# One maximum instruction for the last two score banks, the first keys' bias in the held copy, and the time step's maximum on ScalarE, in a perceiver layer on one core

## Chip, cores and metric

The kernel runs on one core of a Trainium2 chip. The metric is the device time of one execution in microseconds. Profiles are of one execution each. PE is TensorE (PEld its weight loads), DVE is VectorE, ACT is ScalarE, POOL is GpSimd, and SP issues the DMAs.

## The reference, cut to what matters

One perceiver layer in fp32: 16 sequences of 128 queries, width 512, each with a context of 2048 rows. It has three parts, each with a residual sum.

```
# 1. cross attention: 16 heads of 32
q = layernorm(x) @ wq.T + bq;  k = ctx @ wk.T + bk;  v = ctx @ wv.T + bv
attn = softmax(q k^T / sqrt(32));  x = x + (attn @ v) @ wo.T + bo
# 2. a Mamba block (width 1024, 16 states, 128 time steps) and a GELU MLP
dt = softplus(dt_low @ dt_proj_w.T + dt_proj_b)
h  = exp(dt * A) * h + dt * B * xa      # scan over time
# 3. a small mixture of experts
```

What the change touches: the softmax's maxima over the scores, the bias bk of the keys, and softplus, which the kernel computes as max(t, 0) + log(1 + exp(-|t|)) with t = the projection plus its bias.

## The kernel before

**Steps.** The attention runs in 256 steps u (loop at L1329). A step takes one block of 512 context rows of one sequence and one group of four heads: `split(u)` gives the sequence u // 16, the block u // 4 % 4 and the head group u % 4. Its scores are four matmuls (`scores`, L302), one head each, into four PSUM banks of 128x512, `banks[0..3]` (L129). The other four PSUM banks are `avp` (attention sums), `hst` (scan), `pa` and `pc` (products for keys and values).

**Softmax.** `maxima` (L312) reduces each bank on DVE (L315) into one column of its own tile `nm`, and `exps` (L319) follows on ACT with one exponential a bank (L325), which takes the negated maximum as its bias and also sums the row. The maxima are local to a block and are joined at a sequence's end (`joined`, L460). The probabilities of banks 0 and 1 are transposed on PE into the same two banks (`turn`, L353, matmuls at L357) and copied out by ACT (L359); those of banks 2 and 3 are transposed on DVE in blocks (`blocks`, L337) and put in order by DMA through DRAM (L341, L347). The next step's `weighted` (L385) multiplies them with the values.

**Keys and values** of the next block are made in the same steps from seven quarter products (`product`, L244) in place of eight. In step u with u % 4 equal to 1 or 2 it is keys, else values, each in two phases. `x_products` fills `pa` and `pc`. `hold` (L285) copies `pa` to SBUF on ACT; `x_sums` adds `pc` to the held copy on DVE (L264 for keys, with the bias bk, one instruction for each of the two head groups r; L274 for values). Then `y_products` (one product in phase 0, two in phase 1) adds to `pa` and `pc`, and `y_sums` holds or sums again; the fourth quarter is a sum on ACT (L262, bias and copy).

**The scan** of a group of two sequences runs beside later sequences' attention, from step 54 on. `dt_first` (L662) makes the time step of a block of 128 channels in every fourth step, u % 4 = 3, behind the products: a matmul (L665), Abs and Exp on ACT (L669, L670), the maximum on DVE (L672), a sum on POOL. `decays` (L719) are exponentials on ACT into `hst`, half of them before the maxima and half after the held copy; `scan` (L734, L735) runs on DVE and POOL.

**Order.** Each engine's order is the order of the calls in the loop; nothing rearranges it. Waits are put in by tile: a write to a tile waits for the last reads of it, whichever part these read. In a step the order is: half of the decays; scores; `weighted` of the step before; maxima; `x_products`; exps; POOL's work; first scan; hold; second half of the decays; blocks; `x_sums`; `turn` for banks 0 and 1; second scan (before the late work in even steps, after it in odd ones); late work; `y_products` and `y_sums`; work put behind.

**Late work** (L1421 to L1443) is a list of functions that need a PSUM bank for a while, such as `scaled` (L499: spreads the softmax's sums over the partitions by transposes at L502, then a product on DVE at L507 or L509; two in the step with u % 16 = 3 and two with u % 16 = 4), `x_part` and `z_part` (L581, L602: the Mamba input projection, matmuls at L577, one of each in eight steps of 32), `x_proj` (L631), `projected` (L762), `turned` (L429, transposes at L432) and `queries`. They get bank 2 first, then bank 3, then bank 0. A single late item in steps with u % 16 = 3 or 10 is put ahead of `turn` (L1430), into bank 2.

From step 256 on no attention is left: the last scans go on beside the MLP and the experts of the sequences already done, then these alone.

Of the kernel before, what the change touches and what calls it, by code (L numbers as in the profile page):

```python
# [19 lines left out]
SB = S // 512  # L20
# [12 lines left out]
NP = 4 - ND  # L33
# [3 lines left out]
def perceiver_layer(ctx: ExitStack, tc: tile.TileContext, a: dict, out: bass.AP):  # L37
    nc = tc.nc
# [74 lines left out]
    with ExitStack() as es:  # L113
        acon = es.enter_context(tc.tile_pool(name="acon", bufs=1))
        keep = es.enter_context(tc.tile_pool(name="keep", bufs=2))
        ssm = es.enter_context(tc.tile_pool(name="ssm", bufs=2))
        psum = es.enter_context(tc.tile_pool(name="psum", bufs=1, space=PSUM))
        att = es.enter_context(ExitStack())
        pool = att.enter_context(tc.tile_pool(name="att", bufs=2))
# [6 lines left out]

        banks = [psum.tile([P, 512], FP, tag=f"s{j}", name=f"bank{j}") for j in range(4)]  # L129
        avp = psum.tile([P, 4, P], FP, tag="av", name="avp")  # L130
        hst = psum.tile([P, NH // 2, GT], FP, tag="h0", name="hst")
        pa = psum.tile([P, 2, 256], FP, tag="pa", name="pa")
        pc = psum.tile([P, 2, 256], FP, tag="pc", name="pc")

        bq = acon_in("bq", [P, KC])
        bk = acon_in("bk", [P, KC])
# [116 lines left out]
        def k_sum(g, o, c, pc, x):  # L253
            for r in range(2):
                hg = 2 * o + r
                if (g, hg) not in kts:
                    kts[g, hg] = pool.tile(
                        [P, 512], FP, tag=f"kt{hg}", name=f"kt{g}_{hg}", bufs=1 + (hg == 3)
                    )
                t = kts[g, hg][:, c * 256 : (c + 1) * 256]  # L260
                if pc is None:
# [17 lines left out]
            for i, ps in (((1, pa), (2, pc)), ((7, pa), (5, pc)))[ph]:  # L279
                product(of, g, i, ps)  # L280

        def hold(key, g, pa, tag):
            n = ND if tag == "tr" else 1
            t = pool.tile([P, 2 * n, 256], FP, tag=tag, name=f"{tag}{key}{g}", bufs=1)[:, 0:2, :]
            nc.scalar.copy(t, pa)  # L285
            held[key] = t

        def x_sums(of, g, ph, pa, pc):
# [5 lines left out]

        def y_sums(of, g, ph, pa, pc, tag="u2"):
            if ph == 0:
                hold(of + "u2", g, pa, tag)
            else:
                sums[of](g, 0, 1, pc, held[of + "u2"])
                sums[of](g, 1, 0, None, pa)  # L300

        def scores(u):  # L302

            b, sb, hg = split(u)
            for j in range(4):
# [4 lines left out]
            del kts[u // 4, hg]  # L310

        def maxima(u):  # L312
            b, sb, hg = split(u)
            for j in range(4):
                nc.vector.tensor_reduce(  # L315
                    stats[b][0][j][:, sb, hg : hg + 1], banks[j], AX.X, ALU.max, negate=True
                )

        def exps(u):  # L319
            b, sb, hg = split(u)  # L320
            nm, sm = stats[b]
            pr = pool.tile([P, 4, 512], FP, tag="pr", name=f"pr{u}", bufs=1)
            for j in range(4):
                h = hg * 4 + j
                nc.scalar.activation(  # L325
                    pr[:, j, :],
                    banks[j],
                    AF.Exp,
                    bias=nm[j][:, sb, hg : hg + 1],
                    accum_out=sm[:, sb, h : h + 1],  # L330
                )
            prs[u] = pr
# [81 lines left out]
        def normal(b):  # L414

            x = xts[b]
            root_third(rstd[:, b : b + 1], *xts.pop((b, "r")))
            xn = keep.tile([P, D], FP, tag="aT", name="xn", bufs=1)
            nc.vector.tensor_scalar(
                xn, x, mv[:, b, 0:1], rstd[:, b : b + 1], ALU.subtract, ALU.mult  # L420
            )
            if b:
                nc.gpsimd.tensor_tensor(x, x, bo, ALU.add)
            xts[b, "n"] = xn
            nm = [keep.tile([P, SB, 4], FP, tag=f"nm{j}", name=f"nm{b}_{j}") for j in range(4)]
            sm = keep.tile([P, SB, H], FP, tag="sm", name=f"sm{b}")
            stats[b] = nm, sm

# [31 lines left out]
        def joined(b):  # L460

            parts, sm = stats[b]
            nm = keep.tile([P, SB, H], FP, tag="nm", name=f"nm{b}")
            for j in range(4):
                nc.vector.tensor_copy(
                    nm.rearrange("p s (k j) -> p s k j", j=4)[:, :, :, j], parts[j]
                )
            stats[b] = nm, sm

        def joined_first(b):  # L470
# [191 lines left out]
        def dt_first(g, ec, ps):  # L662

            ps = ps[:, 0:GT]
            nc.tensor.matmul(ps, dtw, xd, start=True, stop=True)  # L665


            e = ssm.tile([P, GT], FP, tag="e", name="e", bufs=1)
            nc.scalar.activation(e, ps, AF.Abs, bias=dtb[:, ec : ec + 1])  # L669
            nc.scalar.activation(e, e, AF.Exp, scale=-1.0)  # L670
            dt = ssm.tile([P, GT], FP, tag="dt", name="dt")
            nc.vector.tensor_scalar(dt, ps, dtb[:, ec : ec + 1], 0.0, ALU.add, ALU.max)  # L672
            u = ssm.tile([P, GT], FP, tag="u", name="u", bufs=1)
            nc.gpsimd.tensor_scalar(u, e, 1.0, 1.0, ALU.mult, ALU.add)
            dts[g, ec] = dt, e, u
# [124 lines left out]
        def flat(ps):  # L800
            return ps.rearrange("p k q -> p (k q)")
# [6 lines left out]
        def give_back(*ps):  # L808
            free_banks.extend(ps)
# [466 lines left out]

        def first_sums(of, ph):
            sa, sc = dict((w[0], w[1:3]) for w in ways)[of]
            hold(of, 0, sa, "u1")
            x_sums(of, 0, ph, sa, sc)  # L1280

        load_factors("k", 1, ("a11",))
# [46 lines left out]
        for u in range(last):  # L1329
# [47 lines left out]
            if u == NU:  # L1377
                weighted(NU, range(NP, 4))
                weighted_last(u - 1)
                att.close()  # L1380
                give_back(*banks, flat(avp))
                open_ffn()
            if u == NU + 8:
# [22 lines left out]
            if live and u % 4 == 2:  # L1406
                values_kept(u // 4)
            if makes:
                hold(of, made, pa, "u1")
            if scans:  # L1410
                decays(g, r, 1)
            if live:
# [6 lines left out]


            after_turns = late.get(u, ())  # L1421
            free = banks[NP:]
            places = [(free + banks)[i] for i in range(len(after_turns))]
            if live and len(after_turns) > len(free):
                if u % 4 == 0:
                    places = [flat(avp), *places[:-1]]
                elif u % 2 and makes and u not in behind:
                    places[-1] = flat(pc)
# [110 lines left out]
```

## Time and profile before

| | us |
|---|---|
| median of 3 runs | 3578.6 (3576.97 to 3579.74) |
| the profiled execution | 3579.3 |
| its span, first to last instruction | 3577.5 |
| PE busy | 3518.9 |
| DVE busy | 2672.0 |
| POOL busy | 2462.7 |
| ACT busy | 2285.5 |
| 1024 maxima of a bank (L315), mean of one | 0.678 |
| 1024 exponentials of a bank (L325), mean of one | 0.684 |
| held copies (L285), 128x512, mean of one | 0.58 to 0.60 |
| sums of keys (L264), 128x256, mean of one | 0.46 to 0.48 |
| sums of values (L274), 128x512, mean of one | 0.66 to 0.69 |
| the time step's maximum (L672), 128x256, mean of one | 0.476 |

The granted TensorE clock is 0.995 of full speed. The steps 0 to 255 begin at 43.1 us and the last begins at 2888.1 us.

How to read it: a line of the timeline gives the start in us from the span's start, the duration, the engine, the source line, the operation, the tiles (out<-in), the shapes and, with x, how many follow each other; in brackets stands how long the engine sat idle before and what released it. Matmuls are pipelined and their ends are modelled, so the row of a matmul reaches into the next one. A line of the table of windows gives a stretch, its length, and the busy time and instructions of PE, PEld, DVE, ACT and POOL, then the granted clock, the DMA share and the DMA rate.

### The profile page before, as it was taken

The numbers are of one execution on the slowest core, as the hardware profiler recorded it, in microseconds if no ns is written. First come the engines' busy times: TensorE is split into PE (matmuls) and PEld (weight loads), VectorE is DVE, ScalarE is ACT, GpSimd is POOL, SyncE is SP. The second block draws the span as 40 slices with busy tenths as digits, with TensorE's granted clock in tenths as the row PEclk, the third lists the DMA queues.
The fourth block names the chain that finished last, engine by engine and source line by source line (L and its number), as shares of the span: only waits on it lengthen the run. The fifth ranks groups of instructions, "written<-read, shape, count | busy, mean of one in ns | idle before, by whom it ended". The sixth has DMA issues, their size and how long they took to land.

```text
span 3577.5 us, 68547 instructions
## 1 busy us (share of the span) xinstructions
PE 3518.9 (98%) x24072; PEld 2638.5 (74%) x24072; DVE 2672.0 (75%) x4390; ACT 2285.5 (64%) x5672; POOL 2462.7 (69%) x2353
## 2 busy tenths in 40 slices
PE   8999999999999999999999999999999989999999
PEld 6777787778777877787778777877777756656655
DVE  4555556897889788978797879887988767668743
ACT  3555556777677766777677767776777665545422
POOL 2111214896889788978797779777987778789920
PEclk9999999999999999999999999999999999999999
DMA  4444445787788778787788778778777887676742
GB/s 146 159 148 154 159 152 193 250 265 220 254 251 268 233 253 256 252 243 247 250 257 247 231 257 265 240 224 271 254 245 224 266 300 254 219 273 245 260 173 77
DMA packets 527541, 816.79 MB, mean 228 GB/s; under 512 B 44848, under 2 KB 378960, under 8 KB 526944
## 3 DMA queue, kind: packets, MB, share of 16 engines
q1 hardware_dynamic: 526752, 811.79, 70.4%
q8 instruction: 192, 3.15, 0.3%
q14 instruction: 149, 1.22, 0.1%
q0 software_dynamic: 448, 0.63, 0.1%
HBM read 661.51 MB, written 150.73 MB: 227 GB/s over the span
## 4 chain that ended last, share of the span: by engine, by line
PE 86%; DVE 4%; POOL 4%; DMA 3%; ACT 3%; issue 1%; SPq 0%; DVEq 0%; POOLq 0%
PE pa L244 24%; PE pc L244 17%; PE bank L307 7%; PE avp L385 7%; PE bank L577 6%; PE bank L357 6%; PE bank L986 3%; PE bank L762 3%; PE bank L955 2%; PE bank L1087 2%; PE bank L515 2%; ACT pr L325 1%; POOL w L698 1%; DMA bc<-bcd 1%; PE bank L442 1%
## 5 line engine op out<-in xcount | busy, mean ns | idle before, releaser
L325 ACT ACTIVATE pr<-bank,nm 128x512 f32<-128x512 f32 x1024 | 688.5, 684 | 199.3 <-DVE nm L315 197.3
L315 DVE TENSOR_REDUCE nm<-bank 128x1 f32<-128x512 f32 x1024 | 633.8, 678 | 60.0 <-PE bank L307 59.6
L698 POOL TENSOR_TENSOR w<-dx,bc 128x512 f32<-128x512 f32 x512 | 648.1, 1287 | 30.7 <-DMA bc<-bcd 22.6
L749 POOL TENSOR_TENSOR ysum<-ysum,w 128x512 f32<-128x512 f32 x384 | 500.4, 1303 | 229.4 <-DVE hst L712 205.9
L719 ACT ACTIVATE hst<-dt,alog 128x254 f32<-128x254 f32 x918 | 442.4, 482 | 71.5 <-DVE hst L712 39.1
L337 DVE STREAM_TRANSPOSE tr<-pr 128x1024 f32<-128x1024 f32 x256 | 318.8, 1245 | 119.9 <-ACT pr L325 110.3
L735 POOL TENSOR_TENSOR w<-w,bc 128x512 f32<-128x512 f32 x256 | 329.1, 1286 | 76.6 <-DVE w L734 74.0
L385 PEld LDWEIGHTS avp<-pT,v 128*32 128x32 f32 x4096 | 204.4, 110 | 198.3 <-issue 194.2
L734 DVE TENSOR_TENSOR_SCAN w<-hst,w 128x512 f32<-128x512 f32 x256 | 309.5, 1209 | 40.0 <-ACT hst L719 33.2
L236 POOL TENSOR_TENSOR t<-c,c 128x512 f32<-128x512 f32 x128 | 164.3, 1283 | 232.3 <-PE pc L244 135.6
L359 ACT COPY pT<-bank 128x512 f32<-128x512 f32 x512 | 271.7, 581 | 48.9 <-PE bank L357 48.8
L307 PE MATMUL bank<-kt,qT 32*128 32x512 f32 x2048 | 301.3, 641 | 1.6 <-ACT pT L359 1.6
L385 PE MATMUL avp<-pT,v 128*32 128x128 f32 x4096 | 276.4, 277 | 1.5 <-ACT pT L359 1.4
L357 PE MATMUL bank<-ident,pr 128*128 128x128 f32 x2048 | 266.2, 273 | 0.8 <-ACT pr L325 0.7
L357 PEld LDWEIGHTS bank<-ident,pr 128*128 128x128 f32 x2048 | 239.1, 141 | 27.7 <-ACT pr L325 2.5
L734 DVE TENSOR_TENSOR_SCAN hst<-hst,w 128x512 f32<-128x512 f32 x203 | 247.8, 1221 | 7.1 <-ACT hst L719 7.1
L244 PE MATMUL pa<-t,ks 128*128 128x256 f32 x1024 | 248.6, 386 | 0.0
L244 PE MATMUL pa<-vs,t 128*128 128x256 f32 x1008 | 244.8, 386 | 0.0
L577 PE MATMUL bank<-zT,win 128*128 128x256 f32 x992 | 224.8, 379 | 0.0
L244 PEld LDWEIGHTS pa<-t,ks 128*128 128x128 f32 x1024 | 185.9, 190 | 36.0 <-issue 13.8
L244 PEld LDWEIGHTS pa<-vs,t 128*128 128x128 f32 x1008 | 183.0, 190 | 35.6 <-ACT hst L719 9.9
L385 PE MATMUL avp<-pd,v 128*32 128x128 f32 x3072 | 205.8, 276 | 3.2 <-DMA pd<-trd 3.2
(315 smaller groups left out, 7709.8 us busy)
## 6 DMA issues: line engine op xcount, KB each, us to landing
bc<-bcd SPq DMA_DIRECT2D x512, 512.0 KB, 5.3
trd<-tr SPq DMA_DIRECT2D x256, 512.0 KB, 3.8
pd<-trd SPq DMA_DIRECT2D x1024, 128.0 KB, 2.9
c<-in_ctxT_dram SPq DMA_DIRECT2D x256, 256.0 KB, 6.0
wf<-in_w_dram SPq DMA_DIRECT2D x124, 512.0 KB, 6.7
wqo<-in_wqkvo_dram SPq DMA_DIRECT2D x128, 256.0 KB, 6.3
win<-in_win_dram SPq DMA_DIRECT2D x128, 256.0 KB, 5.9
wout<-in_wout_dram SPq DMA_DIRECT2D x128, 256.0 KB, 6.2
```

The source lines that it names most:

```text
L244: nc.tensor.matmul(ps[:, r, :], l[:, kc, r * P : (r + 1) * P], m[:, kc, :], start=(i in (1, 2, 5) and r == 0 and kc == 0), stop=(r == 1 an ...
L307: nc.tensor.matmul(banks[j], qts[b][rows, hg, :], kts[u // 4, hg][rows, :], start=True, stop=True)
L315: nc.vector.tensor_reduce(stats[b][0][j][:, sb, hg : hg + 1], banks[j], AX.X, ALU.max, negate=True)
L325: nc.scalar.activation(pr[:, j, :], banks[j], AF.Exp, bias=nm[j][:, sb, hg : hg + 1], accum_out=sm[:, sb, h : h + 1],)
L357: nc.tensor.transpose(ps[:, i, :], prs[u][:, j, i * P : (i + 1) * P], ident)
L385: nc.tensor.matmul(avp[j * HD : (j + 1) * HD, v % 4, :], values(v, i, j), pts[v, j][:, i, :] if j < NP else pds[v][:, :, j - NP, i, :], st ...
L577: nc.tensor.matmul(ps, w[:, kc, :], zTs[g][:, kc, :], start=(kc == 0), stop=(kc == KC - 1))
L698: nc.gpsimd.tensor_tensor(w, dx.unsqueeze(1).to_broadcast([P, NH // 2, GT]), bcs[g * 32 + r, 0][:, i * NH // 2 : (i + 1) * NH // 2, :], AL ...
L719: nc.scalar.activation(bt(h[:, k, :])[:, :, 1:], bt(dt)[:, :, 1:], AF.Exp, scale=aneg[:, ec, n : n + 1],)
L734: nc.vector.tensor_tensor_scan(y if i else x, y, x, 0.0, ALU.mult, ALU.add)
L735: eng.tensor_tensor(w, to, bcs[g * 32 + r, DS][:, i * NH // 2 : (i + 1) * NH // 2, :], ALU.mult)
L749: nc.gpsimd.tensor_tensor(s, s, w, ALU.add)
```

## The change

Three edits, with what they bring along.

1. Banks 2 and 3 become the two halves of one tile `pair` [128, 2, 512]. `maxima` reduces banks 0 and 1 as before and both halves of `pair` with one instruction, which writes two columns. The tile of these maxima has a last axis of 2, so `joined` copies three tiles and not four. A write to `pair` waits for reads of either half. The places of the late work change from banks 2, 3, 0, 1 to 2, 0, 1, 3. After the attention, banks 2 and 3 are made anew as single tiles.
2. The keys of head groups 0 and 1 share one tile `kt01`. Where these keys are summed, `hold` adds the bias on ACT (two activations of 128x256, since the bias differs by head group), and DVE adds both groups with one tensor_tensor of 128x512 without a bias.
3. In `dt_first` the maximum with 0 is a Relu with bias on ACT, behind the Exp.

```
-        banks = [psum.tile([P, 512], FP, tag=f"s{j}", name=f"bank{j}") for j in range(4)]
+        banks = [psum.tile([P, 512], FP, tag=f"s{j}", name=f"bank{j}") for j in range(2)]
+        pairs = att.enter_context(tc.tile_pool(name="pairs", bufs=1, space=PSUM))
+        pair = pairs.tile([P, 2, 512], FP, tag="s23", name="pair")
+        banks += [pair[:, 0, :], pair[:, 1, :]]
...
         def k_sum(g, o, c, pc, x):
...
+                    if o == 0:
+                        t = pool.tile([P, 2, 512], FP, tag="kt01", name=f"kt{g}_01", bufs=1)
+                        kts[g, 0], kts[g, 1], kts[g, "01"] = t[:, 0, :], t[:, 1, :], t
...
+                if o == 0:
+                    if r == 0:
+                        nc.vector.tensor_tensor(
+                            kts[g, "01"][:, :, c * 256 : (c + 1) * 256], pc, x, ALU.add
+                        )
+                elif pc is None:
...
-        def hold(key, g, pa, tag):
+        def hold(key, g, pa, tag, biased=False):
...
-            nc.scalar.copy(t, pa)
+            if biased:
+                for r in range(2):
+                    nc.scalar.activation(
+                        t[:, r, :], pa[:, r, :], AF.Identity, bias=bk[:, r : r + 1]
+                    )
+            else:
+                nc.scalar.copy(t, pa)
...
-                hold(of + "u2", g, pa, tag)
+                hold(of + "u2", g, pa, tag, of == "k")
...
         def maxima(u):
             b, sb, hg = split(u)
-            for j in range(4):
+            for j in range(2):
                 nc.vector.tensor_reduce(
                     stats[b][0][j][:, sb, hg : hg + 1], banks[j], AX.X, ALU.max, negate=True
                 )
+            nc.vector.tensor_reduce(
+                stats[b][0][2][:, sb, hg, :], pair, AX.X, ALU.max, negate=True
+            )
...
-                    bias=nm[j][:, sb, hg : hg + 1],
+                    bias=nm[2][:, sb, hg, j - 2 : j - 1] if j > 1 else nm[j][:, sb, hg : hg + 1],
...
-            nc.vector.tensor_scalar(dt, ps, dtb[:, ec : ec + 1], 0.0, ALU.add, ALU.max)
+            nc.scalar.activation(dt, ps, AF.Relu, bias=dtb[:, ec : ec + 1])
...
-            hold(of, 0, sa, "u1")
+            hold(of, 0, sa, "u1", of == "k" and ph == 0)
...
+                singles = es.enter_context(tc.tile_pool(name="singles", bufs=1, space=PSUM))
+                banks[2:] = [
+                    singles.tile([P, 512], FP, tag=f"s{j}", name=f"bank{j}") for j in (2, 3)
+                ]
...
-                hold(of, made, pa, "u1")
+                hold(of, made, pa, "u1", of == "k" and phase == 0)
...
-            free = banks[NP:]
-            places = [(free + banks)[i] for i in range(len(after_turns))]
-            if live and len(after_turns) > len(free):
+            free = [banks[2]]
+            places = [banks[2], banks[0], banks[1], banks[3]][: len(after_turns)]
+            if live and len(after_turns) > 2:
```

More of the change, by code (lines that the diff above doesn't have):

```diff
@@ L256, in k_sum @@
                 if (g, hg) not in kts:
-                    kts[g, hg] = pool.tile(
-                        [P, 512], FP, tag=f"kt{hg}", name=f"kt{g}_{hg}", bufs=1 + (hg == 3)
-                    )
-                t = kts[g, hg][:, c * 256 : (c + 1) * 256]
-                if pc is None:
+                    if o == 0:
+                        t = pool.tile([P, 2, 512], FP, tag="kt01", name=f"kt{g}_01", bufs=1)
+                        kts[g, 0], kts[g, 1], kts[g, "01"] = t[:, 0, :], t[:, 1, :], t
+                    else:
+                        kts[g, hg] = pool.tile(
+                            [P, 512], FP, tag=f"kt{hg}", name=f"kt{g}_{hg}", bufs=hg - 1
+                        )
+                t = kts[g, hg][:, c * 256 : (c + 1) * 256]
+                if o == 0:
[4 more added lines that the diff above has]
+                elif pc is None:
                     nc.scalar.activation(t, x[:, r, :], AF.Identity, bias=bk[:, hg : hg + 1])
@@ L280, in x_products @@
                 product(of, g, i, ps)
-        def hold(key, g, pa, tag):
+        def hold(key, g, pa, tag, biased=False):
             n = ND if tag == "tr" else 1
             t = pool.tile([P, 2 * n, 256], FP, tag=tag, name=f"{tag}{key}{g}", bufs=1)[:, 0:2, :]
-            nc.scalar.copy(t, pa)
+            if biased:
[3 more added lines that the diff above has]
+                    )
+            else:
+                nc.scalar.copy(t, pa)
             held[key] = t
@@ L310, in scores @@
             del kts[u // 4, hg]
+            kts.pop((u // 4, "01"), None)
         def maxima(u):
             b, sb, hg = split(u)
-            for j in range(4):
+            for j in range(2):
                 nc.vector.tensor_reduce(
@@ L317, in maxima @@
                 )
+            nc.vector.tensor_reduce(
+                stats[b][0][2][:, sb, hg, :], pair, AX.X, ALU.max, negate=True
+            )
         def exps(u):
@@ L424, in normal @@
             xts[b, "n"] = xn
-            nm = [keep.tile([P, SB, 4], FP, tag=f"nm{j}", name=f"nm{b}_{j}") for j in range(4)]
+            nm = [
+                keep.tile([P, SB, 4, 2] if j == 2 else [P, SB, 4], FP, tag=f"nm{j}", name=f"nm{b}_{j}")
+                for j in range(3)
+            ]
             sm = keep.tile([P, SB, H], FP, tag="sm", name=f"sm{b}")
@@ L463, in joined @@
             nm = keep.tile([P, SB, H], FP, tag="nm", name=f"nm{b}")
[L464 to L467, printed above, removed]
+            for j in range(3):
+                to = nm.rearrange("p s (k j) -> p s k j", j=4)
+                nc.vector.tensor_copy(to[:, :, :, 2:4] if j == 2 else to[:, :, :, j], parts[j])
             stats[b] = nm, sm
@@ L1380, in perceiver_layer @@
                 att.close()
+                singles = es.enter_context(tc.tile_pool(name="singles", bufs=1, space=PSUM))
+                banks[2:] = [
+                    singles.tile([P, 512], FP, tag=f"s{j}", name=f"bank{j}") for j in (2, 3)
+                ]
                 give_back(*banks, flat(avp))
```

## The prediction

> **What bounds the kernel now.** I read the page first: the busy times and the chain that ended last.
>
> ```profile
> span 3577.5 us, 68547 instructions
> ...
> PE 3518.9 (98%) x24072; PEld 2638.5 (74%) x24072; DVE 2672.0 (75%) x4390; ACT 2285.5 (64%) x5672; POOL 2462.7 (69%) x2353
> ...
> PE 86%; DVE 4%; POOL 4%; DMA 3%; ACT 3%; issue 1%; SPq 0%; DVEq 0%; POOLq 0%
> ```
>
> PE holds the chain. A busy PE could still hide gaps, so I next took the table of windows, cut at the starts of single steps (columns: length, then busy time of PE, PEld, DVE, ACT, POOL).
>
> ```profile
> 1993.90:2002.24 8.34, 8.34 (x74) 6.43 (x73) 8.10 (x12) 6.06 (x17) 8.05 (x8) 1.00 0.52 172
> ...
> 2017.12:2026.76 9.64, 9.64 (x84) 7.68 (x83) 9.03 (x14) 5.83 (x16) 6.90 (x6) 1.00 0.60 199
> ...
> 2101.65:2114.04 12.39, 10.95 (x85) 8.33 (x84) 12.12 (x20) 8.09 (x20) 9.65 (x11) 1.00 0.65 213
> ```
>
> Most steps are as long as their matmuls, to the hundredth; the third waits 1.43 us. Windows over the stage of the 256 live steps (43 to 2888 us) give PE 555.09 of 557, 596.41 of 600, 794.82 of 800 and 877.03 of 888: idle 21.7 us. That is all that any relief of another engine can win there. So the question is not how much work DVE loses, but whether what PE waits for comes later. After 2888 us PE is busy for 660 of 689 us.
>
> **Where the maxima stand in a step.** The timeline of the third of these steps (start, duration, engine, line):
>
> ```profile
> 2106.00 2.47 DVE L315 TENSOR_REDUCE nm<-bank 128x1 f32<-128x512 f32 x4
> 2106.71 0.69 ACT L325 ACTIVATE pr<-bank,nm 128x512 f32<-128x512 f32 x1 [1.98 <-DVE nm L315]
> ...
> 2108.05 0.69 ACT L325 ACTIVATE pr<-bank,nm 128x512 f32<-128x512 f32 x1
> ...
> 2108.71 0.69 ACT L325 ACTIVATE pr<-bank,nm 128x512 f32<-128x512 f32 x1
> 2108.88 0.66 PE L432 MATMUL bank<-ident,xn 128*128 128x128 f32 x4 [1.43 <-ACT pr L325]
> ...
> 2109.68 0.60 ACT L285 COPY u1k<-pa 128x512 f32<-128x512 f32 x1
> ...
> 2110.42 0.45 PE L244 MATMUL pa<-t,ka 128*128 128x256 f32 x1
> ```
>
> Four maxima take 2.47 us, one 678 ns, so each starts 0.60 after the last. The exponentials follow one by one: the third starts 2.05 after the first maximum, and ScalarE then runs without a gap into the held copy, after which PE's next product into pa can start (copy ends 2110.28, product 2110.42). L432 writes bank 2 and starts 0.14 after the third exponential ends (2108.74).
>
> **Part 1, one maximum for two banks.** No row has a reduction of 1024 elements. From below: a reduction of 64 elements (L474) took 0.25, one of 512 took 0.678, which is 0.955 ns an element, so 1.17 for 1024. From above: two of the present, 1.36; a bare bound below is 0.68, if width cost nothing. I take 1.2, near the slope. DVE then needs 1.2+1.2 instead of 2.47, 0.07 less a step. But the third exponential waits for both banks: first maximum + 1.19 + 1.2 + 0.04 = 2.43, against 2.05. It starts 0.38 later wherever ScalarE is waiting for DVE. Where ScalarE comes late itself the delay vanishes: in every fourth step it waits for PE (L397) and begins 0.9 after the first maximum is done (2029.51 against 2028.59), and in the step after it waits at L404.
>
> [...]
>
> **Part 2, bias in the held copy.** In one step of four both held copies (u1, u2 of k, phase 0) become two Identity activations. L262 has them: two take 0.85, the copy 0.60, so +0.25 on ScalarE, twice in 64 blocks: 32 us of ScalarE work. DVE's two L264 (0.88) become one addition like L274 (0.65): 0.2 less, 128 times. The maxima of the step after the second such sum start at once behind it, so 0.2 comes off there until the scores' end (1.16 after the step's start) is the limit.
>
> **Part 3, Relu on ScalarE.** 64 instructions of 0.47 (L672) leave DVE, and 64 of 0.42 to 0.48 (rows L670, L669) join ScalarE. They stand before the wait at L397, which has 0.26 idle; ScalarE moves on 0.33 to 0.37 after such an activation, so about 0.1 of lateness is left at most. DVE's maxima start up to 0.47 earlier in these steps, which just pays for part 1's 0.38. The built program has as many activation table loads as before (65), so no reload is added.
>
> [...]
>
> **Part 4, what the pair does to the late work.** In the built program a write to bank 2 waits for the last exponential of the pair, so for bank 3's too, 0.66 later. And the second late item goes to bank 0, which must first be copied out (L359), instead of bank 3. This step is tight now:
>
> ```profile
> 2022.76 1.04 PE L357 MATMUL bank<-ident,pr 128*128 128x128 f32 x8
> ...
> 2023.55 1.06 ACT L359 COPY pT<-bank 128x512 f32<-128x512 f32 x2
> 2023.63 1.04 PE L502 MATMUL bank<-ident,fx 128*128 128x128 f32 x8
> ...
> 2024.50 0.38 PE L244 MATMUL pa<-vs,t 128*128 128x256 f32 x1
> ```
>
> PE goes from the transposes (L357) over the late work (L502, two items of 0.43) into the next product without a gap. The second item starts at 2024.07; the copy of bank 0, the first of the two L359, ends at 2024.13 by its own row.
>
> **The sum.** The steps repeat with a period of 32. I took the one from u=160 (1797 to 2164 us), read each start and end from the timeline, and moved each producer by the above; PE resumes about 0.15 after its producer ends (2108.74 to 2108.88).
> - Scaled sums (L502) in bank 0: step at 2017.12: copy 2024.13 + 0.23 (0.38, less 0.15 of earlier maxima) + 0.15 against 2024.07: 0.44. Step at 1825.16: much the same, 0.42. Step at 2026.76: copy ends 2034.15, +0.05 +0.15 against 2033.71: 0.6. Step at 1834.80: as much, but the step after waits 0.98 for DVE (L509) now, which does not move: 0. Together 1.46.
> - x and z parts (L577): step at 1980.39: x now waits for bank 3's exponential (+0.4), then z for bank 0's copy (9.05 after the step's start, +0.15, against 8.24 now): 0.95 in all. The two steps from 1887.81, where the copy ends at 7.69 and 7.99 and moves 0.55 (with the bias) and 0.4: 0.15 and 0.3. Together 1.4.
> - L432 in the step at 2101.65: third exponential +0.38, and bank 3's instead: 1.07 later; the product behind it, which waited for the copy, 0.8 later.
> - Held copy before the product in steps without late work (PE needs it by 6.35): step at 1815.06: 6.33 now, +0.25 (0.38 less earlier maxima), 0.23; at 1993.90: 6.07 now, +0.25 for the bias and 0.12, 0.09. Together 0.3.
> - Nothing: the x projection (2008.97), which ends on POOL's xa anyway, and the steps with ScalarE late.
>
> 3.96 us a period, six times (steps 54 to 255 hold the scans): 23.8. Six scalings before step 54 at 0.12, one held copy at step 250 at 0.4: 24.9. Every wait that DVE's relief could shorten I found unmoved within 0.1. The end after 2888 us keeps its POOL chain: eight Relu of the last group move 3.8 us of DVE there, which I set at 0, at most 3 either way. The profiled execution took 3579.3 (span 3577.5 and 1.8 around it), 0.7 above the median of the runs shown, so 3579.3 + 24.9 = 3604.
>
> **Rivals.**
> - *Heavier (3618).* The wide maximum costs 1.36: 0.16 more at nine sites a period, six times, is 9; then held copies in plain steps miss 6.35 too (5.82 + 0.54 in the step at 1868.55 just reaches it), about 0.8 a period, 5. For it: two banks in one instruction. Against: the slope.
> - *Covered (3584).* The maximum is cheap, under 0.82, where the third exponential is not late (1.19 + 0.82 + 0.04 = 2.05). Left are the late items' bank 0 and bank 3's exponential, about 0.8 a period: +5. Against: it would have to run at twice the rate of L315.
> - *Relief reaches PE (3568, faster).* Place: the maxima's start in steps where DVE is late (3.45 after the start in the step at 2075.16, where PE waits 0.5 for the held copy). If DVE's 0.47 and 0.2 come off these and the third exponential is not late, half of PE's 21.7 us go: -11. Decides from the same 0.82. For it: 197.3 us of ScalarE's idle time are put down to the maxima. Against: nearly all of that is beside a busy PE.
>
> **How the numbers follow.** Forecast 0.62 (own range 3592 to 3619), heavier 0.12, covered 0.14, relief 0.12. The measurement tells about 0.2%, 7 us, from no change: slower 0.74, same 0.14, faster 0.12. The range 3580 to 3626 takes in the covered case and the heavier one, and leaves out the faster.
>
> **What will show it.** Right: PE's idle time in the live stage goes from 22 to about 47 us; waits of L502's successor for ScalarE's copy, some 20 times near 0.5, that are not there now; PE's wait for the exponentials at L432's successor from 1.43 to about 2.5; DVE about 65 us less busy, ScalarE 60 more; the wide maximum near 1200 ns. Wrong: steps of 9.64 and 10.93 us stay as they are (bank 0 costs nothing), the reduction is under 0.82 or near 1.36, or the difference lies after 2888 us.

## The result, and the profile after

The changed kernel takes 3633.0 us (median of 4 runs, 3631.4 to 3635.8) beside 3577.9 of the kernel before on the same chip: 1.0154 times as long, interval 1.0137 to 1.0172. That is +55 us where +25 was forecast. The page of the changed kernel, the first lines and the chain that ended last:

```profile
span 3629.7 us, 68322 instructions
...
PE 3532.6 (97%) x24072; PEld 2641.3 (73%) x24072; DVE 2618.7 (72%) x3926; ACT 2356.1 (65%) x5864; POOL 2462.6 (68%) x2353
...
PE 71%; DVE 10%; ACT 8%; POOL 4%; issue 4%; DMA 3%; SPq 0%; DVEq 0%; POOLq 0%
```

DVE lost 53 us of work and ACT gained 71. PE's share of the chain fell from 86% to 71%, and DVE and ACT took it over. The loss lies in the stage of the live steps (first to last start): 2902.0 us, before 2845.0. The start is 1.3 us shorter and the end 3.6.

The table of windows for the three steps that the prediction showed, and for one that it did not (step 90; columns as there: length, busy PE, PEld, DVE, ACT, POOL, granted clock, DMA):

```profile
2028.57:2036.94 8.37, 8.37 (x74) 6.46 (x73) 7.48 (x9) 6.09 (x18) 8.13 (x10) 1.00 0.48 153
2051.90:2062.76 10.86, 9.83 (x84) 7.66 (x83) 9.72 (x12) 5.95 (x16) 6.17 (x6) 1.00 0.58 190
2139.01:2152.23 13.22, 10.72 (x85) 8.30 (x84) 12.20 (x20) 8.79 (x22) 9.97 (x12) 1.00 0.69 221
1010.49:1025.38 14.89, 12.40 (x86) 9.66 (x85) 12.20 (x20) 9.30 (x23) 11.56 (x13) 0.89 0.66 222
```

The first step is 0.03 longer than before. The second went from 9.64 to 10.86, more than the 0.44 of the forecast, and PE idles in it. The third went from 12.39 to 13.22, the 0.8 of the forecast. The fourth holds the same work as the third (before, 12.40) but takes 14.89, and its clock is below 1.

The third step's timeline in the changed kernel answers to the lines shown of before:

```profile
2143.37 1.28 DVE L334 TENSOR_REDUCE nm<-bank 128x1 f32<-128x512 f32 x2
2144.09 0.69 ACT L347 ACTIVATE pr<-bank,nm 128x512 f32<-128x512 f32 x1 [1.98 <-DVE nm L334]
2144.57 1.21 DVE L337 TENSOR_REDUCE nm<-pair 128x2 f32<-128x1024 f32 x1
...
2145.81 0.69 ACT L347 ACTIVATE pr<-pair,nm 128x512 f32<-128x512 f32 x1 [0.28 <-DVE nm L337]
...
2147.32 0.65 PE L457 MATMUL pair<-ident,xn 128*128 128x128 f32 x4 [2.50 <-ACT pr L347]
```

The wide maximum takes 1.21, the third exponential waits 0.28 for it, and PE waits 2.50 for the last one: all as worked out.

Now the step at 1825.16 (before), 1855.72 (after), where the forecast had +0.42 and the step grew by 1.40. First the timeline of before, DVE and POOL ahead of the maxima:

```profile
1826.06 0.45 DVE L620 SCALAR_TENSOR_TENSOR sg<-zs,sg 128x256 f32<-128x256 f32 x1
1826.18 1.46 POOL L735 TENSOR_TENSOR w<-w,bc 128x512 f32<-128x512 f32 x1
...
1826.43 2.47 DVE L315 TENSOR_REDUCE nm<-bank 128x1 f32<-128x512 f32 x4
```

Then the changed kernel's timeline of the same step:

```profile
1856.34 1.27 POOL L759 TENSOR_TENSOR w<-w,bc 128x512 f32<-128x512 f32 x1
1856.43 1.47 DVE L644 SCALAR_TENSOR_TENSOR sg<-zs,sg 128x256 f32<-128x256 f32 x1
...
1857.82 1.27 DVE L334 TENSOR_REDUCE nm<-bank 128x1 f32<-128x512 f32 x2
...
1863.32 1.06 ACT L381 COPY pT<-bank 128x512 f32<-128x512 f32 x2
...
1864.04 0.63 PE L526 MATMUL bank<-ident,fx 128*128 128x128 f32 x4 [1.21 <-ACT pT L381]
```

DVE's instruction for the gate (`silu_second`, two inputs in SBUF) stands ahead of the maxima on DVE. Before, it started 0.12 ahead of POOL's product and took 0.45; POOL's took 1.46 in place of 1.27. Now PE is later by 0.4 (the step before has grown by 0.41) but POOL is not, so POOL starts 0.09 ahead of DVE, and DVE's instruction takes 1.47. The maxima start 2.10 after the step's start and not 1.27, everything behind them comes later, and at the end of that line PE waits 1.21 for the copy of bank 0, where the second late item goes now. The groups by tile of the gate instruction (min/median/max in ns), before and then changed:

```profile
L620 DVE SCALAR_TENSOR_TENSOR sg<-zs,sg x64: 414/760/1517, 585.9 to 3398.7; 128x256 f32<-128x256 f32 x64
```

```profile
L644 DVE SCALAR_TENSOR_TENSOR sg<-zs,sg x64: 416/1406/1491, 587.0 to 3449.4; 128x256 f32<-128x256 f32 x64
```

Its median went from 0.76 to 1.41 us. The same turn stands in the steps at 2051.90 and 2074.34: POOL is under way when the gate starts, the gate takes 1.29 and 1.45 in place of 0.51 and 0.71, and the steps grow by 1.22 and 0.71, the last one a step that the forecast put at nothing. So the theory is: **the pair's waits are about as large as forecast, but by moving PE and POOL against each other by tenths of a microsecond (PE 0.4 later in the step shown) they turn the order of starts between DVE and POOL, and DVE is then held for most of a POOL instruction in front of the maxima.** A second term is the halved clock behind the long gap. The rivals: ScalarE's 71 us of added work; the width of the maximum; bank 0; or the later exponentials alone.

### The profile page after: what moved, and what is told of

It reads as the page before. It is cut to its first block, busy times and chain, and to the rows that moved or that the text cites. A ratio compares the mean times of both kernels' runs of the same rounds, so it can differ in the third digit from the quotient of the medians.

```text
span 3629.7 us, 68322 instructions
## 1 busy us (share of the span) xinstructions
PE 3532.6 (97%) x24072; PEld 2641.3 (73%) x24072; DVE 2618.7 (72%) x3926; ACT 2356.1 (65%) x5864; POOL 2462.6 (68%) x2353
## 3 DMA queue, kind: packets, MB, share of 16 engines
q14 instruction: 149, 1.22, 0.1%
## 4 chain that ended last, share of the span: by engine, by line
PE 71%; DVE 10%; ACT 8%; POOL 4%; issue 4%; DMA 3%; SPq 0%; DVEq 0%; POOLq 0%
PE pa L247 18%; PE pc L247 12%; PE bank L325 5%; PE avp L407 5%; ACT pr L347 4%; PE bank L379 4%; PE bank L1010 4%; PE bank L601 3%; PE bank L979 2%; PE bank L1111 2%; PE pair L601 2%; PE pair L786 2%; DVE nm L334 2%; DVE nm L337 2%; PE pair L539 2%
## 5 line engine op out<-in xcount | busy, mean ns | idle before, releaser
L722 POOL TENSOR_TENSOR w<-dx,bc 128x512 f32<-128x512 f32 x512 | 646.7, 1284 | 19.1 <-DMA bc<-bcd 10.7
L347 ACT ACTIVATE pr<-bank,nm 128x512 f32<-128x512 f32 x512 | 346.9, 682 | 208.1 <-DVE nm L334 206.7
L334 DVE TENSOR_REDUCE nm<-bank 128x1 f32<-128x512 f32 x512 | 328.5, 682 | 84.2 <-PE pair L325 77.2
L759 POOL TENSOR_TENSOR w<-w,bc 128x512 f32<-128x512 f32 x256 | 327.7, 1280 | 81.2 <-DVE w L758 76.5
L347 ACT ACTIVATE pr<-pair,nm 128x512 f32<-128x512 f32 x512 | 346.9, 684 | 42.8 <-DVE nm L337 40.8
L337 DVE TENSOR_REDUCE nm<-pair 128x2 f32<-128x1024 f32 x256 | 310.3, 1212 | 0.0
L325 PE MATMUL bank<-kt,qT 32*128 32x512 f32 x1024 | 290.9, 641 | 2.4 <-ACT pT L381 2.0
L325 PE MATMUL pair<-kt,qT 32*128 32x512 f32 x1024 | 289.5, 641 | 0.0
L379 PE MATMUL bank<-ident,pr 128*128 128x128 f32 x2048 | 269.8, 275 | 0.8 <-ACT pr L347 0.7
L379 PEld LDWEIGHTS bank<-ident,pr 128*128 128x128 f32 x2048 | 242.0, 142 | 28.0 <-ACT pr L347 2.5
```

Source lines behind the costliest of these rows:

```text
L325: nc.tensor.matmul(banks[j], qts[b][rows, hg, :], kts[u // 4, hg][rows, :], start=True, stop=True)
L334: nc.vector.tensor_reduce(stats[b][0][j][:, sb, hg : hg + 1], banks[j], AX.X, ALU.max, negate=True)
L337: nc.vector.tensor_reduce(stats[b][0][2][:, sb, hg, :], pair, AX.X, ALU.max, negate=True)
L347: nc.scalar.activation(pr[:, j, :], banks[j], AF.Exp, bias=nm[2][:, sb, hg, j - 2 : j - 1] if j > 1 else nm[j][:, sb, hg : hg + 1], accum_ ...
L379: nc.tensor.transpose(ps[:, i, :], prs[u][:, j, i * P : (i + 1) * P], ident)
L722: nc.gpsimd.tensor_tensor(w, dx.unsqueeze(1).to_broadcast([P, NH // 2, GT]), bcs[g * 32 + r, 0][:, i * NH // 2 : (i + 1) * NH // 2, :], AL ...
```

## The experiments

Each kernel was timed beside the kernel before on the same chip; the second time given is that kernel's median, and a ratio's 95% interval stands in brackets.

### Which part costs

> Part 1 alone (the pair tile, the wide maximum, the places 2, 0, 1, 3); the keys' sums and the time step's maximum as before. Theory P (the pair makes the third exponential 0.38 us late, and late items wait for bank 3's exponential or bank 0's copy): +40 to +60 us against the kernel before, nearly all of the +55, since the other two parts only shift about 0.2 to 0.5 us between DVE and ScalarE. Theory S (ScalarE's added 71 us, the biased copies and the Relu, make PE wait): +20 to +30 us, and the other two parts give the rest.

Measured: 3634.0 beside 3579.5, 1.0147 [1.0134, 1.0161], +54.5. The pair alone is the whole loss.

> Parts 2 and 3 alone (bias in the held copy, Relu on ScalarE); four banks, four maxima and the places as before. Theory P: between -8 and +8 us against the kernel before (DVE's relief comes off steps in which PE does not wait for it, the biased copy costs some 0.1 to 0.4 us in two steps of 32). Theory S: +20 to +35 us, with PE's waits for the held copy u1 and u2 in the steps that make keys.

Measured: 3570.8 beside 3579.5, 0.9973 [0.9962, 0.9985], -8.8, just outside theory P's -8 to +8. ScalarE's added work costs nothing; the rival falls. But this is a gain that the prediction denied.

> The changed kernel, but the pair's two maxima are two instructions of 512 elements, as before; the pair tile, its waits and the places stay. Theory P says that the width does half of the harm: third exponential back at 2.05 us behind the first maximum, PE's gap ahead of the transposes of xn (steps 58, 90 and so on) 2.1 us instead of 2.5, in all +20 to +35 us against the kernel before. If the tile-wide wait and bank 0 do nearly all of it: +45 to +55 us. If the width does nearly all: +0 to +12 us.

```
-            nc.vector.tensor_reduce(
-                stats[b][0][2][:, sb, hg, :], pair, AX.X, ALU.max, negate=True
-            )
+            for j in range(2):
+                nc.vector.tensor_reduce(
+                    stats[b][0][2][:, sb, hg, j : j + 1], pair[:, j, :], AX.X, ALU.max, negate=True
+                )
```

Measured: 3638.1, 1.0161 [1.0147, 1.0175], +58.6: no faster than with the wide maximum (the two intervals overlap). The +20 to +35 missed; the nearest range is the +45 to +55 of the tile-wide wait and bank 0. The edit did not free the third exponential: its trace has it behind the fourth reduction. So the width as such adds nothing.

> The kernel before with one edit: the places of the late items are banks 2, 0, 1, 3 in place of 2, 3, 0, 1; single tiles, four maxima. Theory P: the second late item waits for bank 0's copy by its present lateness alone, without the 0.38 us: 0 to 0.25 us in some six steps of 32, +3 to +15 us against the kernel before. Rival (bank 0's copy is the whole cause): +35 us or more.

Measured: 3587.8, 1.0022 [1.0013, 1.0031], +8.2, inside the range of theory P. Bank 0 by itself is a small term.

### What in the pair costs

> The kernel before, four banks and four maxima, one edit: the third and the fourth maximum go to one tile with two columns, so the third exponential waits for the fourth maximum's end, 0.46 us later than now; places, sums and the time step as before. Theory L (what costs is that the exponentials, and so DVE's and ScalarE's work behind them, come later in the step): +20 to +35 us against the kernel before. Theory T (what costs is that a write to bank 2 waits for reads of bank 3 and the other way round): +3 to +12 us.

Measured: 3574.1 beside 3579.9, 0.9982 [0.9974, 0.9991], -5.8. Both theories missed, and the edit says nothing on them: in its trace the third exponential still starts 2.05 behind the first maximum, so the shared tile of columns in SBUF did not hold it there. With the gain goes a shorter gate instruction: in the step at 1980 us it falls from 1.47 to 0.41. The likely reason is `joined`, which has three copies and not four to do ahead of it there; that was not tried by itself.

> The pair tile and the places 2, 0, 1, 3, but four maxima into four tiles, so the third exponential is released by the third maximum as before; sums and time step as before. Theory L: +10 to +22 us against the kernel before (places +8, the wait for bank 3's exponential ahead of the transposes of xn 0.7 us in six steps). Theory T: +38 to +52 us, near the +54 of the pair with the wide maximum.

```
+        pair = pairs.tile([P, 2, 512], FP, tag="s23", name="pair")
+        banks += [pair[:, 0, :], pair[:, 1, :]]
...
             for j in range(4):
                 nc.vector.tensor_reduce(
                     stats[b][0][j][:, sb, hg : hg + 1], banks[j], AX.X, ALU.max, negate=True
                 )
```

Measured: 3646.5, 1.0187 [1.0173, 1.0201], +66.6, above both ranges and the slowest so far. The timeline of the step at 2146.76 tells why it is no test of an early third exponential:

```profile
2152.31 1.27 DVE L318 TENSOR_REDUCE nm<-pair 128x1 f32<-128x512 f32 x2
...
2153.62 0.69 ACT L328 ACTIVATE pr<-pair,nm 128x512 f32<-128x512 f32 x1 [0.35 <-DVE nm L318]
```

The third exponential reads the half that the third reduction has done, yet ScalarE sits idle for 0.35 us and the fourth reduction, which reads the other half, releases it. So in this run too, with no wide maximum, the pair makes three waits: a later third exponential, a first late item behind the last exponential, and (by the places) a second behind bank 0's copy. The next two rebuild these waits without a pair.

> The kernel before, one edit: the maxima are taken in the order of banks 0, 1, 3, 2, so the third exponential is released by the fourth reduction, 0.46 us later than now (the separate tile of columns did not move it); four single banks, places as before. If the later exponentials alone make the loss: +40 to +60 us against the kernel before. If they need a late item that waits for the last exponential or for bank 0's copy: -3 to +12 us.

```
-            for j in range(4):
+            for j in (0, 1, 3, 2):
```

Measured: 3594.6 beside 3580.4, 1.0043 [1.0030, 1.0056], +14.3, a little above the -3 to +12 of the second answer, far from the +40 to +60 of the first.

> The kernel before with the same order of maxima and the late items' places 3, 0, 1, 2 in place of 2, 3, 0, 1: what the pair does to the waits (third exponential 0.46 us late, first late item behind the last exponential, second behind bank 0's copy), with four single banks and four maxima. If these three waits are the whole of the pair's effect: +45 to +70 us against the kernel before, beside +67 for the pair with four maxima. If something else in the pair's tile costs: under +30 us.

```
-            for j in range(4):
+            for j in (0, 1, 3, 2):
...
+            free = [banks[3]]
+            places = [banks[3], banks[0], banks[1], banks[2]][: len(after_turns)]
```

Measured: 3649.1, 1.0193 [1.0179, 1.0207], +68.7. Four single banks, four maxima, and the pair's loss is all there. Summed over the steps from 54 on, its trace differs from that of the pair with four maxima by 0.0 us. Windows of the step that was 9.64 before, first with the later exponentials alone, then with the places too:

```profile
1832.70:1842.34 9.64, 9.64 (x84) 7.68 (x83) 9.15 (x13) 7.13 (x19) 9.56 (x12) 1.00 0.76 269
```

```profile
1863.19:1874.23 11.04, 9.84 (x83) 7.67 (x83) 9.90 (x14) 7.14 (x19) 10.96 (x13) 1.00 0.79 264
```

In both the gate instruction takes 1.22 there and the maxima start 2.04 after the step's start. Alone, that is hidden (9.64, as before); with an item that needs bank 0's copy it reaches PE. The later exponentials cost 14 alone, the places 2, 0, 1, 3 cost 8 alone; with both kinds of wait in one kernel it is 69. The third wait, of the first late item for the last exponential, comes in only with the two together and was not tried alone.

### Taking the hold away

> The changed kernel with one edit: DVE's small instruction for the gate (sg<-zs,sg, two SBUF inputs) stands behind the next step's maxima instead of ahead of them. In the changed kernel it takes 1.3 to 1.5 us where POOL's w<-w,bc has just started (0.45 in the kernel before) and shifts all that follows. If that phase is a part of the loss: 8 to 20 us less than the changed kernel, +35 to +47 us against the kernel before, with steps of the kinds 3 and 21 of 32 back by 0.8 us or more. If the maxima stand late for other reasons: within 4 us of the changed kernel (+51 to +59).

```
             if live:
                 maxima(u)
+                silu_second()
...
-            silu_second()
+            if not u + 1 < NU:
+                silu_second()
```

Measured: 3582.6 beside 3579.9, 1.0012 [1.0003, 1.0020], +2.7. One instruction's place takes some 50 of the 55 us back, where 8 to 20 were expected. The step of the 1.40, in this kernel's timeline:

```profile
1829.39 1.28 POOL L759 TENSOR_TENSOR w<-w,bc 128x512 f32<-128x512 f32 x1
...
1829.95 1.29 DVE L334 TENSOR_REDUCE nm<-bank 128x1 f32<-128x512 f32 x2 [0.36 <-PE pair L325]
...
1832.28 0.92 DVE L644 SCALAR_TENSOR_TENSOR sg<-zs,sg 128x256 f32<-128x256 f32 x1
...
1836.18 0.63 PE L526 MATMUL bank<-ident,fx 128*128 128x128 f32 x4 [0.28 <-POOL w L722]
```

POOL's product is under way at the maxima's start as before, but the two reductions, which read PSUM, take 1.29 beside it (1.27 in the changed kernel), and PE idles 0.28 ahead of the late item in place of 1.21. The step is 0.47 longer than in the kernel before; 0.42 was forecast.

> The kernel before with one edit: DVE's instruction for the gate stands behind the next step's maxima. If the move is worth 50 us only because the changed kernel let POOL's instruction start ahead of it: -12 to 0 us against the kernel before (one gate a period, 1.47 us in the step at 1980 us, is slow here). If the move is worth as much by itself: -20 us or less, near the floor set by 22 us of idle PE.

Measured: 3573.3 beside 3580.4, 0.9977 [0.9968, 0.9986], -7.1. So the move by itself is worth 7 and not 50: it pays where the pair's waits have let POOL start first.

> Parts 2 and 3 alone, with the same move of DVE's instruction for the gate behind the maxima. If the phase against POOL matters only where the exponentials are late: within 3 us of parts 2 and 3 alone, -6 to -12 us against the kernel before. If it costs there too: -13 to -20 us.

Measured: 3570.0 beside 3579.9, 0.9972 [0.9961, 0.9983], -10.0, beside -8.8 for parts 2 and 3 alone: there the move brings no gain clear of the noise.

> The changed kernel with one edit: POOL's additions and products over 128x512 are two instructions of 128x256 each, except w<-dx,bc. If DVE's gate instruction is held for as long as the POOL instruction under way (in the records it ends 0.28 us behind POOL's end), then where a half is under way (0.73 us for 128x256) it takes at most 1.02 us, and the median of sg<-zs,sg falls from 1.41 to 1.0 or less; the time, with some 0.2 us more of POOL's work for each pair of halves, goes anywhere from -25 to +20 us against the changed kernel. If the gate's length does not hang on POOL's instruction: median 1.3 or more, as now.

```
-                nc.gpsimd.tensor_tensor(s, s, w, ALU.add)
+                for k in range(2):
+                    nc.gpsimd.tensor_tensor(s[:, k, :], s[:, k, :], w[:, k, :], ALU.add)
```

(so too the other sums and L759). Measured: 3640.7 beside 3579.0, 1.0173 [1.0156, 1.0190]. The gate's group in it:

```profile
L647 DVE SCALAR_TENSOR_TENSOR sg<-zs,sg x64: 415/784/2216, 585.7 to 3459.3; 128x256 f32<-128x256 f32 x64
```

The median fell from 1.41 to 0.78: the hold got shorter with the instruction that holds. The 40 gates that start while one of 128x256 is under way take 1.00 at most, inside the 1.02 expected; in the changed kernel 53 start under one of 128x512 and take up to 1.49. In the step of the 1.40 the gate takes 1.11 and not 1.47, but what holds it there is w<-dx,bc, which was left whole and is further on when the gate starts. The longest, three of 2.2, were not expected at all: they are held through two w<-dx,bc in a row.

The gate is still ahead of the maxima here, so three steps of a period (1825.16, 2017.12 and 2037.69 in before) part the hold from the gate's own 0.42. Where the gate takes 1.11 in place of 1.47, 0.97 in place of 1.29 (in the three periods without the 2.2) and 0.42 in place of 1.45, the step is 0.36, 0.32 and 0.68 shorter than in the changed kernel; the last is then 0.03 longer than in the kernel before. That step's timeline in the changed kernel:

```profile
2075.06 1.45 DVE L644 SCALAR_TENSOR_TENSOR sg<-zs,sg 128x256 f32<-128x256 f32 x1
2076.43 0.68 DVE L334 TENSOR_REDUCE nm<-bank 128x1 f32<-128x512 f32 x1
```

And with POOL's halves (the step starts at 2074.34 there and at 2077.99 here):

```profile
2078.71 0.42 DVE L647 SCALAR_TENSOR_TENSOR sg<-zs,sg 128x256 f32<-128x256 f32 x1
...
2079.15 0.69 DVE L335 TENSOR_REDUCE nm<-bank 128x1 f32<-128x512 f32 x1
```

Unheld in its place, the gate lets the maxima start 1.16 after the step's start, as with the gate moved behind them: in this step the hold is the whole cost. Yet the time as a whole did not fall, and this timeline shows the main reason:

```profile
1879.67 2.77 POOL L783 TENSOR_TENSOR ysum<-ysum,w 128x256 f32<-128x256 f32 x4
1879.70 3.02 DVE L706 SCALAR_TENSOR_TENSOR e<-u,e 128x256 f32<-128x256 f32 x1
```

An instruction of DVE with two SBUF inputs starts 0.03 behind the first of four POOL instructions that follow each other without a gap, and ends 0.28 behind the last: held for 3.02 us, through all four. That step grows by 2 us in each period, and the three steps with a gate of 2.2 by 2.6. POOL's halves that stood back to back did not let DVE in between.

### The long gap of PE

> The changed kernel with one edit: the single late item of the steps 58, 90 and so on (transposes of xn) goes behind the transposes of banks 0 and 1 and not ahead of them, so PE does not sit 2.5 us for bank 3's exponential. If the halved clock follows from that gap: no stretch of 3.4 us at half clock is left in these steps, they are 1.5 to 3 us shorter each, 9 to 18 us less than the changed kernel, +37 to +46 us against the kernel before. If the clock drops for another reason, or the wait only moves: within 5 us of the changed kernel.

```
-            ahead = live and u % 16 in (3, 10) and len(after_turns) == 1
+            ahead = live and u % 16 == 3 and len(after_turns) == 1
```

Measured: 3624.9 beside 3580.4, 1.0124 [1.0110, 1.0138], +44.5. By the ratios it is 10.7 less than the changed kernel, at the low end of the 9 to 18. In the traces the steps of this kind are 8.8 shorter in sum, and no stretch of half clock is left in steps 2 to 253, as expected. The changed kernel's timeline of the step at 1010.49, behind the gap:

```profile
1018.79 0.66 PE L457 MATMUL pair<-ident,xn 128*128 128x128 f32 x4 [2.49 <-ACT pr L347]
...
1019.28 1.65 PE L379 MATMUL bank<-ident,pr 128*128 128x128 f32 x8
...
1020.72 3.00 PE L247 MATMUL pa<-t,ka 128*128 128x256 f32 x8
```

In the step at 2139.01 the gap is as long (2.50), but the eight transposes (L379) take 1.04 there. The table of windows of the two stretches behind the gap gives the clock:

```profile
1019.60:1022.90 3.30, 3.30 (x13) 2.85 (x12) 3.27 (x6) 2.16 (x5) 2.77 (x5) 0.50 0.66 210
2148.10:2150.20 2.10, 2.10 (x15) 1.92 (x14) 2.10 (x5) 2.07 (x5) 2.10 (x3) 1.00 0.46 189
```

> The changed kernel with the gate's instruction behind the maxima and the transposes of xn behind the other transposes. PE's gap ahead of them is 1.6 us with the first edit alone and causes no half clock there, so the second edit has less to win than the 8 us that it won in the changed kernel: -2 to -8 us against the first edit alone, that is -5 to +1 us against the kernel before. If the two edits add up: -6 to -10 against the kernel before or better.

Measured: 3587.8 beside 3579.5, 1.0022 [1.0012, 1.0032], +8.3, not the -5 to +1 expected. Where the gap is short (1.6 us) and the clock stays, moving the transposes of xn wins 0.1 a step and loses 0.6 in the next. So what the edit won in the changed kernel was mostly the clock.

### The gain of parts 2 and 3, and a version that beats both

> Part 3 alone, the time step's maximum on ScalarE. In the step at 1980 us the gate instruction on DVE started 0.07 us behind POOL's w<-dx,bc and took 1.47 us; without the 0.47 of the maximum ahead of it it starts first. If that phase makes the gain of parts 2 and 3: the gate in this step at 0.4 to 0.7, the step with the x projection 0.9 to 1.0 us shorter, -4 to -8 us against the kernel before. If the gain is DVE's 30 us less work anywhere: -2 to +2.

Measured: 3570.9 beside 3579.5, 0.9977 [0.9969, 0.9986], -8.6, a little more than the -4 to -8 of the phase.

> Part 2 alone, the bias of the first keys in the held copy. If the phase of the one gate makes the gain of parts 2 and 3: -3 to +3 us against the kernel before, since this part does not shorten DVE's work ahead of that gate. If the fewer sums on DVE make it: -5 to -10.

Measured: 3579.6, 1.0001 [0.9991, 1.0010]. All the gain is the Relu's, and most of it hangs on one phase. The timeline of before in the step at 1980.39:

```profile
1982.03 0.47 DVE L672 TENSOR_SCALAR dt<-pc,dtb 128x256 f32<-128x256 f32 x1
...
1982.36 2.67 POOL L698 TENSOR_TENSOR w<-dx,bc 128x512 f32<-128x512 f32 x2
1982.43 1.47 DVE L620 SCALAR_TENSOR_TENSOR sg<-xa,sg 128x256 f32<-128x256 f32 x1
```

And with the Relu on ScalarE:

```profile
1978.63 0.62 DVE L620 SCALAR_TENSOR_TENSOR sg<-xa,sg 128x256 f32<-128x256 f32 x1
...
1978.95 2.65 POOL L698 TENSOR_TENSOR w<-dx,bc 128x512 f32<-128x512 f32 x2
```

The gate lost that race by 0.07 us before and wins it by 0.32 now. Two steps on, the x projection, which waits for POOL's xa, comes 0.97 earlier in each of six periods: 5.8 of the 6.5 us that the live stage wins. Moving the gate alone (before_silu) shortens the same step by 1.07.

> A version meant to beat both: parts 2 and 3, the gate's instruction behind the maxima, and the transposes of xn behind the transposes of banks 0 and 1; single banks, four maxima. By the steps of the runs before, the last edit has at most the 1.3 us of PE's idle time in six steps to win: -10 to -17 us against the kernel before. If PE's wait there moves to another producer: -8 to -11, as without it.

Measured: 3573.7 beside 3579.5, 0.9985 [0.9976, 0.9994], -5.8, outside both ranges: no better than without the last edit. Three kernels, parts 2 and 3 alone, the Relu alone, and parts 2 and 3 with the gate moved, stand at 3570 to 3571; all beat the kernel before by 0.2 to 0.3%, and with it the changed one, and their intervals do not tell them apart.

## Why the prediction was wrong, point by point

Direction, place and mechanism of the waits were right; the size was not: a full period of 32 steps grew by 7.1 to 9.7 us in place of 3.96. By its steps:

- **The wide maximum, 1.2.** Right: 1.212 (256 of them). The rivals that hang on 1.36 or on 0.82 fall.
- **Third exponential 0.38 later.** Right: 0.40 (6.80 after the step's start, before 6.40). The cause is wider than named: with narrow maxima in a pair (pair_split) the fourth reduction releases the third exponential too, after 0.35 of idle ScalarE.
- **Scaled sums, 0.44, 0.42 and 0.6.** With the hold out of the way (the gate behind the maxima) these steps grew by 0.47, 0.47 and 0.64. In the changed kernel they grew by 1.22, 1.40 and 0.65. The step at 2037.69, behind the last of them, was put at nothing and grew by 0.71, and by 0.02 with the gate moved.
- **x and z parts, 0.95, 0.15 and 0.3.** In the changed kernel 0, 0.56 and 1.39. The 0.95 did not come since the gate there fell from 1.47 to 0.41 (in mimic, where it stays at 1.47, that step grew by 1.49). In the last the slow one is another DVE instruction ahead of the maxima (L441, xn<-x, 1.65 in place of 0.90); in two periods it takes 0.55, and the step grew by 0.3.
- **L432's step, 0.8.** Exactly that in step 186 (0.82), but 2.2 to 2.5 in four of the other steps of this kind, by the halved clock.
- **Held copies, 0.23 and 0.09.** 0.41 and 0.03, and 0.37 in a step (167) that was put at nothing. The 0.41 is the one that lets POOL start first in the next step.
- **Scaled sums at 1834.80, 0.** +0.65, of which 0.28 come back in the next step, and 0.96 with the hold gone: the wait for L509 was there, as said.
- **"Every wait that DVE's relief could shorten I found unmoved within 0.1."** Wrong: the Relu brings 8 to 9 us, and the x projection's wait for POOL's xa, called fixed, moves with POOL.
- **One maximum for two banks, and the Relu's price.** DVE is 53 us less busy and the kernel is slower; the pair alone is +54.5, so the wide instruction saved no time, but breaking the wide maximum up again (narrow, +58.6) brought nothing back. The Relu on ScalarE gives 8.6, by what it took from DVE's order and not by its price (0.46 there, the maximum 0.48 on DVE).
- **DVE 65 less busy, ScalarE 60 more.** 53 and 71. The group of the gate instruction alone went from 51.4 to 78.0 us on DVE.
- **The end, 0, at most 3.** 3.6 us shorter; over the 19 traces of this study it runs from 685.8 to 692.4, so this is no more than kernels differ there anyway.
- **Idle PE in the live stage, 22 to about 47.** 63 (2902.0 less 2838.6 busy), and 15 more of busy: for instance, at half clock the eight transposes took 1.65 in place of 1.04, and at full clock the 84 matmuls of the step at 2051.90 took 9.83 in place of 9.64.

**The step that failed** is "read each start and end from the timeline, and moved each producer by the above". It moved starts and kept durations. A producer's duration was no constant here: the gate instruction took 0.45 where it started 0.12 ahead of POOL's product and 1.47 where it started 0.09 behind it. The scaled sums came out as worked out once the hold was away; the 51.6 us that the changed kernel takes more in steps 54 to 254 than the version with the gate moved hold what was not in the sum, and some of what was (L432's 0.8 goes too when the gate is moved). Of these some 6 are four stretches of half clock, at about 1.55 each (2.2 to 2.5 against 0.82), and some 6.5 are the gain that the move brings in the kernel before as well. The other 39 go with the gate's place ahead of the maxima. Some 14 of them fall in the three steps of a period where the halved POOL instructions show the hold as the cost (2.4 us in each of six periods). In the rest the hold and the gate's own 0.42, which the move takes off the maxima too, were not parted. No run has every gate unheld in its place, so the sum of 25 as such was not measured.

The row that could have told it was in the trace of before: one form (sg, 128x256), 0.41 at best and 1.5 at worst, while ScalarE's activations on the same tile stay within 0.40 and 0.45. The rows beside it agree: 1.47 against 0.45 for the gate, 1.46 in place of 1.27 for POOL's product where it starts second, and 0.67 to 0.69 for each of the 1024 reductions, with POOL under way or not. That spoke against this change, which moves PE against POOL while such an instruction stands in front of the maxima.

## What to carry to other kernels

When starts are moved on paper, first look for instructions of one form whose durations spread widely: here the gate's length went by a neighbour's start, and a turn of 0.21 us between the two starts added 1.02. Keep such an instruction (here the gate on DVE, 0.42 to 1.49 in the changed kernel, and one with a single wide input, L441, 0.55 to 1.65) out of the stretch that the critical producer waits behind; here its place was worth 50 us in one kernel and 7 in the other. Waits that were cheap one by one (+14 and +8) cost three times their sum in one kernel here (69, with a third wait that only the two together bring), so they are to be tried together too.

## What the runs showed of the hardware

- **How long the gate was held.** In the live stages of before and after, 162 gate instructions start while a POOL tensor_tensor is under way. 154 of them end 0.275 to 0.300 us behind that instruction's end, whatever was left of it. The other eight start within its last 0.08 us and take their own 0.41. With none under way the 52 others take 0.41 to 0.43. Where POOL started second, at 1826.18 in before, 0.12 behind the gate, POOL was the one that was longer (1.46, not 1.27).
- **Held through several instructions.** Four POOL instructions of 128x256 back to back, 2.77 us in all, held DVE for 3.02 us; two w<-dx,bc (some 1.3 each) let DVE in between them at 1982.36 above (the gate ends 0.28 behind the first), but two held it through both for 2.20 us at 920.35 in the kernel with POOL's halves.
- **The half clock behind PE's gaps.** Over steps 2 to 253 of all 19 traces of this study, gaps of PE between 0.7 and 1.2 us were followed by half clock in 0 of 156 cases, 1.2 to 1.9 us in 3 of 95 (all three in the kernel with POOL's halves), and 1.9 to 2.65 us in 25 of 41. Each time it lasted 3.413 us, longer than any of these gaps, and of the five gaps of equal length (2.49 to 2.50 in steps 90 to 218 of the changed kernel) four were followed by it. In each of the 19, all changes of the clock stand whole multiples of 3.413 us apart (to 0.01). Idle time of PE (modelled ends) counted by the stretches of this grid over steps 54 to 253: all 20 with more than 1.98 us are followed by half clock, 8 of 19 between 1.75 and 1.98, and none of the others below. The 2.50 us of the step at 2139.01 are cut by the grid at 2145.94 into 1.1 and 1.4, and nothing follows; the gap in the step at 1010.49 lies within one stretch.
- **Two engines on one PSUM tile.** An exponential on ScalarE of one half was released by a reduction on DVE of the other (0.35 us idle in pair_split above); with two maxima in columns of one SBUF tile (late_third) the third exponential did not start later (2.05 behind the first maximum, as in before).
